# Sine tables from sums of two partial angles, lag matmuls on four column tiles, exponentials first: one change to a two-layer sequence kernel

## The chip, the cores and the metric

The kernel runs on one core of a Trainium2 chip. A core has TensorE (PE; its weight loads are listed as PEld), VectorE (DVE), ScalarE (ACT), GpSimd (POOL) and SyncE (SP), which work through their own instruction streams in order, and 16 DMA engines. DMAs are issued here from the queues of SP, ScalarE and GpSimd. The metric is device time in microseconds (us) for one execution, less is better. Before the change it is 1138.46 us, the median of 7 runs between 1137.23 and 1139.0.

## What is computed

The input `x` has 64 batches, 128 channels and 2048 time steps, in 32-bit floats. Cut to what matters, the reference is

```python
W = weights[condition]                      # one of 16 matrices of 128x128 for each batch
x = x + einsum('bct,bcd->bdt', x, W)        # layer 0
dt = exp(log_dt); A = -exp(log_A_real) + 1j * A_imag; dtA = A * dt[:, None]
Ct = (C[..., 0] + 1j * C[..., 1]) * (exp(dtA) - 1) / A
K = 2 * einsum('hn,hnl->hl', Ct, exp(dtA[:, :, None] * arange(L))).real
y = causal_convolution(x, K) + x * D[:, None]     # by FFT in the reference
x = x + y * mask                            # mask: time step < length of the batch
```

Layer 1 is a linear state-space model: 128 channels h, each with 64 complex modes n. The kernel works with it in chunks of 128 time steps (Q): inside a chunk the output comes from the first 128 values of K as a Toeplitz matrix, and between chunks from states that are carried on.

## The kernel before

It has two stages.

**Stage 1** does layer 0 for the first half of time (1024 steps) and makes the tables of layer 1. A turn of its loop (`now`, 0 to 63) takes one batch (`batch0`, line 464): SP has fetched two batches at a time, 1 MB, into one of ten buffers (`fetch`, line 430; up to nine fetches ahead); GpSimd copies the batch's matrix into a small tile (`weigh`, line 436; three batches ahead, four tiles); TensorE multiplies (`project`, line 448: two matmuls of 512 columns, line 454, into one of two double banks of PSUM); ScalarE copies the result over the input (line 456) and issues its store to a scratch tensor in DRAM (line 459). A buffer is fetched into again when both of its stores have landed. Before turn 12 the parameters of the modes are worked out on DVE, transposed on TensorE (`lay`, line 347) and kept in `gtab`, `ptab` and `wk`; these instructions lie between the first twelve batches, written out by hand.

The tables: the channels are taken in pairs (64 pairs, the two channels' modes on 128 partitions), and pairs in 16 groups of four (TP). For a group `e` holds, for 128 partitions, 4 pairs and 129 steps (NE), the real and imaginary part of a decaying exponential: exp(decay x step) times cosine and sine of an angle. The angle in turns is step x (FHI + FLO) + PHI, where the frequency is kept in two parts for accuracy, and whole turns are taken off by adding and subtracting a large number (MAGIC). The steps of a group in the code:

- `exps` (line 477): four exponentials on ScalarE, 128x129 each. Groups 0 to 3 are done in turns 6 to 9, the others four groups at a time between later batches. Exponentials and sines need different ScalarE function tables; changing them is a table load.
- `angles` (line 590): 16 DVE instructions.
- `sines` (line 617): two ScalarE instructions of 128x516.
- `products` (line 622): two DVE instructions into `e`.
- `lags` (line 631): eight matmuls with weights `wk` of 128x2 and 128 moving columns, which give the 128 lags of K for the group's eight channels as 2 partitions x 4 pairs x 128.
- `keep_lags` (ScalarE copy, line 641), `gain_lags` (line 647, adds 1 + D to lag 0), `store_lags` (line 651, a DMA from GpSimd into the DRAM tensor `kpad`).

From turn 12 on, each turn issues one batch and then six DVE steps of a generator (`tables`, line 688), which goes through the groups as fast as that allows. A small plan (`later`, line 686) places the other engines' steps a fixed number of turns behind. The last groups' steps run over the end of the batches (the loop goes to `B + 9`).

**Stage 2** starts when the scratch tensor is complete: 64 iterations (`iteration`, line 863), each with four channels of one half of time. Per iteration TensorE transposes (line 763), forms the states' inputs (line 788), applies the Toeplitz part (line 829) and the states' part (line 841, on two row tiles of 64 partitions); DVE scans the states (line 803) and writes masked outputs (line 850); SP stores them (`store`, line 856). The second half of layer 0 lies between these as single pieces (`some`, line 662). An iteration's two stores are issued in the iteration after it; those of the last one after the loop.

Of the kernel before, what the change touches and what calls it, by code (L numbers as in the profile page):

```python
# [45 lines left out]
P = 128  # L47
# [16 lines left out]
TP = 4  # L64
# [305 lines left out]
def cond_resid_ssm_kernel(  # L370
# [30 lines left out]
    KP = 2 * Q  # L401
    assert sum(SEGS) == L and set(SEGS) == {SL} and KK == 4
# [11 lines left out]
    kpad = dram.tile([C, KP], F32, tag="kpad", name="kpad")  # L414
    btd = dram.tile([NG, P, GP * 4 * N], F32, tag="btd", name="btd")
# [70 lines left out]
    drow = earlies.tile([2, NP], F32, tag="drow", name="drow")  # L486
# [3 lines left out]
    with tc.tile_pool(name="setup", bufs=1) as setup:  # L490
# [25 lines left out]
        li = setup.tile([P, 1], I32, tag="li", name="li")  # L516
        with nc.allow_non_contiguous_dma(reason="128 gains and 64 lengths"):
            nc.scalar.dma_start(
                drow.rearrange("c (j d) -> c j d", d=2), d_in.rearrange("(j c d) -> c j d", c=2, d=2)
            )  # L520
            for f in range(2):
                nc.scalar.dma_start(li[f * B : (f + 1) * B, :], length.rearrange("(b o) -> b o", o=1))
# [4 lines left out]
        nc.gpsimd.iota(ti, [[1, HL]], base=0, channel_multiplier=0)  # L527

# [8 lines left out]
        def masks():  # L537
            V.tensor_scalar(drow, drow, 1.0, None, ALU.add)
            V.tensor_copy(lf, li)
            V.tensor_copy(steps, stepi)  # L540
            yield
            V.tensor_copy(tf, ti)
            yield
            V.tensor_scalar(tf[B:P], tf[B:P], float(HL), None, ALU.add)
            yield
            for s in range(NS):
                if s:
                    V.tensor_scalar(tf, tf, float(SL), None, ALU.add)
                    yield
                V.tensor_scalar(mask[:, s, :], tf, lf, None, ALU.is_lt)  # L550
                yield
# [37 lines left out]

    def angles(g):  # L590

        t = ts[g] = tmps.tile([P, 2, TP, NE], F32, tag="t", name=f"t_{g}", bufs=4)
        a, r = t[:, 0], t[:, 1]
        for i in range(TP):
            V.tensor_scalar(a[:, i, :], steps, par_of(FHI, g, i), None, ALU.mult)
            yield
        V.tensor_scalar(r, a, MAGIC, MAGIC, ALU.add, ALU.subtract)
        yield
        V.tensor_tensor(a, a, r, ALU.subtract)
        yield  # L600
        for i in range(TP):
            V.tensor_scalar(r[:, i, :], steps, par_of(FLO, g, i), par_of(PHI, g, i), ALU.mult, ALU.add)
            yield
        V.tensor_tensor(a, a, r, ALU.add)
        yield
        V.tensor_scalar(r, a, MAGIC, MAGIC, ALU.add, ALU.subtract)
        yield
        V.tensor_tensor(a, a, r, ALU.subtract)
        yield
        V.scalar_tensor_tensor(r, a, -1.0, a, ALU.mult, ALU.max)  # L610
        later(2, sines, g)
        if g % 4 == 3 and g + 1 < NT:
            for k in range(4):
                later(2 + (k + 1) // 2, exps, g + 1 + k)
        yield
# [6 lines left out]
    def products(g):  # L622
        V.tensor_tensor(es[g][:, :, 1, :], ts[g][:, 0], es[g][:, :, 0, :], ALU.mult)
        yield
        V.tensor_tensor(es[g][:, :, 0, :], ts[g][:, 1], es[g][:, :, 0, :], ALU.mult)
        del ts[g]
        for lag, step in ((3, lags), (4, keep_lags), (6, gain_lags), (8, store_lags)):
            later(lag, step, g)
        yield

    def lags(g):

        pk = ks[g] = psp.tile([2, TP, Q], F32, tag="tr", name=f"pk_{g}", bufs=2)
        for i in range(TP):
            for part in range(2):
                w = wk[:, part, g * TP + i, :]
                nc.tensor.matmul(pk[:, i, :], w, es[g][:, i, part, 1:NE], start=(part == 0), stop=(part == 1))  # L637

    def keep_lags(g):
        krow = tmps.tile([2, TP, Q], F32, tag="krow", name=f"krow_{g}", bufs=3)  # L640
        nc.scalar.copy(krow, ks[g])
        ks[g] = krow

    def gain_lags(g):

        last = ks[g][:, :, Q - 1]
        V.tensor_tensor(last, last, drow[:, g * TP : (g + 1) * TP], ALU.add)

    def store_lags(g):
        h0 = 2 * g * TP  # L650
        nc.gpsimd.dma_start(kpad[h0 : h0 + 2 * TP, 0:Q].rearrange("(p c) q -> c p q", c=2), ks.pop(g))
# [32 lines left out]
    plan = {}  # L684

    def later(lag, step, g):
        plan.setdefault(now + lag, []).append((step, g))

    def tables():
        for g in range(NT + 2):  # L690
            if g < NT:
                yield from angles(g)
            elif g > NT:
                yield from [None] * 12
            if g >= 2:
                yield from products(g - 2)

    making = tables()
    for now in range(12, B + 9):
        if now < B:  # L700
            batch0(now)
        for step, g in plan.pop(now, ()):
            step(g)
        for _ in range(6):
            next(making, None)
        if now == 60:
            fetches(FILL)
    assert not plan and next(making, None) is None
# [147 lines left out]
    def store(i):  # L856
        s, g = seg(i)
        for f in range(2):
            t0 = s * SL + f * HL
            nc.sync.dma_start(out[:, g * CG : (g + 1) * CG, t0 : t0 + HL], xs[i][half[f]])  # L860
        del xs[i]

    def iteration(i):
# [29 lines left out]
        for d in range(GP):  # L893
            if i >= 0:
                outputs(i, d)
            if nxt and d == 0:
# [8 lines left out]
    store(NI - 1)  # L905
# [32 lines left out]
```

## Time and profile before

| | |
|---|---|
| median of 7 runs | 1138.46 us |
| the profiled execution, its own time | 1139.5 us |
| its span | 1137.7 us |
| busy: PE / DVE / ACT / POOL | 1081.1 / 843.0 / 692.8 / 216.5 us |
| granted TensorE clock, mean | 0.99 |
| batch 12's matmuls start | 53.1 us |
| batch 63's matmuls end | 199.5 us |
| batch 63's store lands | 203.4 us |
| the scratch tensor's first load is issued | 203.7 us |

Busy shares are means over two stages. In the page's curves a digit is the busy share of one fortieth of the span (28.4 us) in tenths, 9 for 90% or more, so the first seven digits are stage 1. In the window table each row is a stretch of time, with the busy time of each engine in it and the number of instructions. In the chain of work that ended last each line is a start, a duration, and what the end was waiting for at that time; `x8` counts records, and a 32-bit matmul leaves two of them. In the instruction list a name such as `e<-steps,gtab` says what is written from what.

### The profile page before, as it was taken

To read this page: it belongs to the slowest core of one execution; us is meant where nothing else is said; L and a number is where in the kernel's file an instruction comes from. 1 tells how busy PE (TensorE), PEld (TensorE's weight loads), DVE (VectorE), ACT (ScalarE), POOL (GpSimd) and SP (SyncE) were. 2 spreads that over 40 slices of the span, in tenths; PEclk is the share of its full clock that TensorE was granted. 3 is DMA by queue.
4 is the path that set the end of the run, shared out by engine and by line. 5 is a ranking of instruction groups with operands and counts; after the bars stand their busy time and mean duration, and the time that the engine had idled before them with its cause. 6 is when DMAs were issued, how large, how long until landed. Compare 5 with 4: busy or idle time off the path is not lost.

```text
span 1137.7 us, 23806 instructions
## 1 busy us (share of the span) xinstructions
PE 1081.1 (95%) x8586; PEld 792.3 (70%) x8586; DVE 843.0 (74%) x2811; ACT 692.8 (61%) x1117; POOL 216.5 (19%) x376
## 2 busy tenths in 40 slices
PE   5588889899999999999999999999999999999996
PEld 2233334477777777677777778888888888888885
DVE  7598883266766675676576667888888888888886
ACT  3457785766656656666666666566566566556552
POOL 2012212122222212212222211221121121121120
PEclk9799999999999999999999999999999999999998
DMA  8999998999999999999999977777878787778754
GB/s 316 415 398 372 347 353 312 371 334 291 319 297 291 288 298 309 292 287 305 297 278 296 288 220 226 240 225 222 221 237 225 211 243 227 210 243 227 209 163 111
DMA packets 116793, 313.25 MB, mean 275 GB/s; under 512 B 11428, under 2 KB 11684, under 8 KB 108484
## 3 DMA queue, kind: packets, MB, share of 16 engines
q1 hardware_dynamic: 71184, 219.17, 61.9%
q10 hardware_dynamic: 35764, 67.32, 15.9%
q0 software_dynamic: 9728, 25.25, 8.8%
q8 instruction: 68, 1.11, 0.4%
q14 instruction: 49, 0.40, 0.1%
HBM read 164.76 MB, written 146.93 MB: 274 GB/s over the span
## 4 chain that ended last, share of the span: by engine, by line
PE 87%; DMA 6%; ACT 4%; DVE 1%; issue 1%; ACTq 0%; POOLq 0%; POOL 0%; SPq 0%; DVEq 0%
PE y L841 21%; PE y L829 20%; PE v L788 18%; PE p L454 15%; PE tr L763 10%; DMA xb<-in_x_dram 3%; DMA scr<-xb 2%; PE pk L637 2%; PE pb L745 2%; ACT xb L456 1%; ACT e L480 1%; DVE s L803 1%; DMA x<-scr 0%; ACTq L459 0%; ACT L480 0%
## 5 line engine op out<-in xcount | busy, mean ns | idle before, releaser
L803 DVE SCALAR_TENSOR_TENSOR s<-s,ptab 128x128 f32<-128x128 f32 x1792 | 520.6, 344 | 98.0 <-ACT s L793 80.0
L793 ACT ACTIVATE s<-v,ptab 64x512 f32<-64x512 f32 (+1 forms) x512 | 336.0, 656 | 49.9 <-PE v L788 33.6
L829 PEld LDWEIGHTS y<-tt,u 128*128 128x128 f32 x2048 | 263.5, 192 | 80.5 <-issue 67.0
L454 PE MATMUL p<-xb,w 128*128 128x512 f32 x512 | 255.9, 616 | 38.9 <-ACT xb L456 13.6
L829 PE MATMUL y<-tt,u 128*128 128x128 f32 x2048 | 269.9, 275 | 0.1
L841 PEld LDWEIGHTS y<-e,s 64*128 64x128 f32 x4096 | 233.9, 188 | 46.5 <-issue 24.2
L788 PE MATMUL v<-u,bt 128*128 128x512 f32 (+1 forms) x512 | 248.4, 567 | 0.0
L841 PE MATMUL y<-e,s 64*128 64x128 f32 x4096 | 246.7, 275 | 1.4 <-DVE s L803 1.4
L764 ACT COPY u<-tr 128x512 f32<-128x512 f32 x256 | 150.5, 588 | 153.7 <-PE tr L763 127.4
L812 DVE TENSOR_SCALAR s<-s 128x128 f32<-128x128 f32 x448 | 99.1, 221 | 137.3 <-ACT s L793 137.3
L456 ACT COPY xb<-p 128x512 f32<-128x512 f32 (+1 forms) x192 | 139.1, 725 | 99.3 <-PE p L454 84.0
L850 DVE COPY_PREDICATED x<-mask,y 128x1024 f32<-128x1024 uint8 x128 | 166.6, 1302 | 1.1 <-PE y L841 1.0
L454 PEld LDWEIGHTS p<-xb,w 128*128 128x128 f32 x512 | 88.2, 196 | 112.6 <-issue 82.4
L763 PEld LDWEIGHTS tr<-ident,x 128*128 128x128 f32 x1024 | 121.1, 141 | 51.3 <-issue 44.6
L763 PE MATMUL tr<-ident,x 128*128 128x128 f32 x1024 | 155.6, 274 | 1.0 <-DMA x<-scr 1.0
L446 POOL COPY w<-wres 128x128 f32 x128 | 54.0, 422 | 331.7 <-PE p L454 318.8
L731 POOL DMA_DIRECT2D tt<-kpad x64 | 50.6, 790 | 206.6 <-DVE s L803 166.9
L788 PEld LDWEIGHTS v<-u,bt 128*128 128x128 f32 x512 | 79.6, 191 | 13.9 <-issue 13.6
L746 ACT COPY bt<-pb 128x512 f32<-128x512 f32 x32 | 18.8, 586 | 87.3 <-PE pb L745 86.7
L776 POOL DMA_DIRECT2D s<-carry x64 | 45.0, 708 | 128.1 <-PE y L841 114.3
L820 POOL DMA_DIRECT2D carry<-s x64 | 43.8, 729 | 66.7 <-DVE s L803 62.4
L773 POOL MEMSET s<- 128x384 f32 x32 | 14.8, 462 | 150.4 <-DMA carry<-s 68.9
(169 smaller groups left out, 323.4 us busy)
## 6 DMA issues: line engine op xcount, KB each, us to landing
xb<-in_x_dram SPq DMA_DIRECT2D x64, 1024.0 KB, 9.7
scr<-xb ACTq DMA_DIRECT2D x128, 512.0 KB, 8.0
x<-scr SPq DMA_DIRECT2D x64, 1024.0 KB, 9.2
out_dram<-x SPq DMA_DIRECT2D x128, 512.0 KB, 4.8
tt<-kpad POOLq DMA_DIRECT2D x64, 256.0 KB, 6.3
btd<-bt SPq DMA_DIRECT2D x32, 256.0 KB, 7.9
bt<-btd SPq DMA_DIRECT2D x32, 256.0 KB, 4.9
carry<-s POOLq DMA_DIRECT2D x64, 64.0 KB, 7.1
```

What stands on the lines that cost most here:

```text
L446: nc.gpsimd.tensor_copy(w1s[s, b], wres[:, bass.ds(at, 1), :].rearrange("p s d -> p (s d)"))
L454: nc.tensor.matmul(ps[:, k], w1s[s, b], own[:, cols], start=True, stop=True)
L456: nc.scalar.copy(own[:, cols], ps.rearrange("p k t -> p (k t)"))
L763: nc.tensor.transpose(tr[:, k, :], xs[i][:, c, k * Q : (k + 1) * Q], ident)
L764: nc.scalar.copy(u, tr)
L788: nc.tensor.matmul(v[:, 0:nv], w, us[i, n].rearrange("p k r -> p (k r)")[:, 0:nv], start=True, stop=True)
L793: nc.scalar.activation(own[:, 0:nv], v[lanes, 0:nv], AF.Copy, scale=amp)
L803: nc.vector.scalar_tensor_tensor(new[:, d, 0:2], src, factor, own[:, d, 0:2], ALU.mult, ALU.add)
L812: nc.vector.tensor_scalar(old[:, :, 2], old[:, :, 0], -1.0, None, ALU.mult)
L829: nc.tensor.matmul(y[:, k, :], u[:, k, :], tts[i][:, n, :], start=(k == 0), stop=False, skip_group_check=True)
L841: nc.tensor.matmul(ys[i, d][:, c, k, :], st[half[c], d, part, k, :, :].rearrange("p f b -> p (f b)"), e[half[c], pair % TP, part, 0:Q], st ...
L850: nc.vector.copy_predicated(xs[i][:, d::2, :].rearrange("r c (k t) -> r c k t", k=KK), keep_k.unsqueeze(1).to_broadcast([P, 2, KK, Q]), ys ...
```

## The change

Six things change.

1. **Angles as sums.** A step from 0 to 127 is 16a + b. For each pair, 25 partial angles are worked out once for all groups: 8 for the multiples of 16 (with the phase), 16 for 0 to 15, and one for step 128 (`partial_angles`, in turns 12 to 14: nine DVE instructions of up to 128x1600 and a GpSimd memset of 128x2048). For a group, TensorE transposes its partial angles (`turn_parts`), ScalarE copies them (`keep_parts`), and one matmul with a matrix of zeros and ones (`pick`) adds the two right ones for 4 x 128 steps (`add_parts`). `angles` is then four DVE instructions that take off whole turns and make the second table's absolute value. `pick` is made before turn 12 with six more iotas on GpSimd and four more instructions on DVE.
2. **Lags on column tiles.** The weights are 32 columns (16 pairs' weights, of which those of one pair are wanted), and each of the four pairs of a group has its own 32 output partitions; the wanted rows are then picked by two DMAs.
3. **Exponentials first.** All groups left are done in turns 12 to 17, two groups a turn.
4. **A fixed schedule.** From turn 15 on a group starts every second turn, and each step has its lag in turns (`STEPS`); the loop ends with the batches.
5. **D by rows.** Since lags lie on other partitions, the gains are laid out by two DMAs into DRAM and four out of it, on GpSimd's queue between the third and the fourth batch's weights, in place of one on ScalarE's.
6. **The last store in parts.** The last iteration's outputs are stored pair by pair, one half on SP's queue and the other on ScalarE's.

```diff
             for f in range(2):
-                nc.scalar.dma_start(li[f * B : (f + 1) * B, :], length.rearrange("(b o) -> b o", o=1))
+                nc.scalar.dma_start(lens[f * B : (f + 1) * B, :], length.rearrange("(b o) -> b o", o=1))
...
-            nc.scalar.dma_start(
-                drow.rearrange("c (j d) -> c j d", d=2), d_in.rearrange("(j c d) -> c j d", c=2, d=2)
-            )
+            for c in range(2):
+                nc.gpsimd.dma_start(by_row[c], by_channel[c])
+            for i in range(TP):
+                nc.gpsimd.dma_start(dcol[i * NR : (i + 1) * NR, :], dbyrow.rearrange("(h r) -> r h", r=NR))
...
+    def partial_angles(k):
+        own = parts[:, :, 0:NL]
...
+        if k == 0:
+            nc.gpsimd.memset(parts, 0.0)
+            V.tensor_tensor(own, of(FHI, NL), by_l, ALU.mult)
+            V.tensor_scalar(whole, own, MAGIC, MAGIC, ALU.add, ALU.subtract)
+        elif k == 1:
+            V.tensor_tensor(own, own, whole, ALU.subtract)
+            V.tensor_tensor(whole, of(FLO, NL), by_l, ALU.mult)
+        else:
+            V.tensor_tensor(own, own, whole, ALU.add)
...
+    def turn_parts(g):
+        ps[g] = psp.tile([P, P], F32, tag="tr", name=f"pa_{g}", bufs=2)
+        nc.tensor.transpose(ps[g], parts[:, g * TP : (g + 1) * TP, :].rearrange("p i r -> p (i r)"), ident)
+
+    def keep_parts(g):
+        a = tmps.tile([P, P], F32, tag="a", name=f"a_{g}", bufs=2)
+        nc.scalar.copy(a, ps[g])
+
+    def add_parts(g):
+        ps[g] = psp.tile([P, TP, Q], F32, tag="v", name=f"pt_{g}", bufs=2)
+        nc.tensor.matmul(
+            ps[g].rearrange("p i q -> p (i q)"), a, pick.rearrange("p i q -> p (i q)"), start=True, stop=True
+        )
...
     def angles(g):
-        for i in range(TP):
-            V.tensor_scalar(a[:, i, :], steps, par_of(FHI, g, i), None, ALU.mult)
...
-        V.scalar_tensor_tensor(r, a, -1.0, a, ALU.mult, ALU.max)
+        V.tensor_scalar(r[:, :, 1:NE], ps[g], MAGIC, MAGIC, ALU.add, ALU.subtract)
+        V.tensor_tensor(a[:, :, 1:NE], ps.pop(g), r[:, :, 1:NE], ALU.subtract)
+        V.tensor_copy(a[:, :, 0:1], last[:, g * TP : (g + 1) * TP, :])
+        V.tensor_scalar(r.bitcast(I32), a.bitcast(I32), 0x7FFFFFFF, None, ALU.bitwise_and)
...
     def lags(g):
-        pk = ks[g] = psp.tile([2, TP, Q], F32, tag="tr", name=f"pk_{g}", bufs=2)
-        for i in range(TP):
-            for part in range(2):
-                w = wk[:, part, g * TP + i, :]
-                nc.tensor.matmul(pk[:, i, :], w, es[g][:, i, part, 1:NE], start=(part == 0), stop=(part == 1))
+        pk = ks[g] = psp.tile([P, Q], F32, tag="tr", name=f"pk_{g}", bufs=2)
+        pairs = slice(g // 4 * 16, g // 4 * 16 + 16)
+        for part in range(2):
+            for i in range(TP):
+                w = wk[:, part, pairs, :].rearrange("p k c -> p (k c)")
+                nc.tensor.matmul(
+                    pk[i * NR : (i + 1) * NR, :], w, es[g][:, i, part, 1:NE], start=(part == 0), stop=(part == 1)
+                )
...
     def store_lags(g):
-        nc.gpsimd.dma_start(kpad[h0 : h0 + 2 * TP, 0:Q].rearrange("(p c) q -> c p q", c=2), ks.pop(g))
+        for c in range(2):
+            r0 = g % 4 * 8 + c
+            nc.gpsimd.dma_start(to[c], krow[r0 : r0 + 3 * 34 + 1 : 34, :])
...
-    for now in range(12, B + 9):
-        if now < B:
-            batch0(now)
-        for step, g in plan.pop(now, ()):
-            step(g)
-        for _ in range(6):
-            next(making, None)
+    FIRST = 15
+    STEPS = {12: store_lags, 10: gain_lags, 8: keep_lags, 7: lags, 6: products,
+             4: sines, 3: angles, 2: add_parts, 1: keep_parts, 0: turn_parts}
+    for now in range(12, B):
+        batch0(now)
+        if now < FIRST:
+            partial_angles(now - 12)
+        if now < 18:
+            exps(2 * now - 20)
+            exps(2 * now - 19)
+        for lag, step in STEPS.items():
+            g, odd = divmod(now - FIRST - lag, 2)
+            if not odd and 0 <= g < NT:
+                step(g)
...
-    def store(i):
+    def store(i, d=None):
         s, g = seg(i)
-        for f in range(2):
+        own = slice(0, CG) if d is None else slice(d, CG, 2)
+        for f, queue in ((0, nc.sync), (1, nc.sync if d is None else nc.scalar)):
             t0 = s * SL + f * HL
-            nc.sync.dma_start(out[:, g * CG : (g + 1) * CG, t0 : t0 + HL], xs[i][half[f]])
-        del xs[i]
+            queue.dma_start(out[:, g * CG : (g + 1) * CG, t0 : t0 + HL][:, own], xs[i][half[f], own])
...
             if i >= 0:
                 outputs(i, d)
+            if not nxt:
+                store(i, d)
...
-    store(NI - 1)
```

In turn n the steps stand behind the batch, oldest group first, so a group's first transpose is in turn 15 + 2g, its angle matmul in turn 17 + 2g, its lag matmuls in turn 22 + 2g and its stores in turn 27 + 2g; the last stores are in turn 57.

## The prediction

> **What bounds the kernel now.** I read the two-line load curve first, then a table of time windows, then the chain that ended last, then the instructions of one stretch in order of time. Everything the change touches, the last store apart, lies in stage 1, which ends when batch 63's store has landed (203.4 us). After it TensorE is the bound.
>
> ```profile
> PE   5588889899999999999999999999999999999996
> DMA  8999998999999999999999977777878787778754
> ```
>
> DMA is nearly full in stage 1 too, so the question is which of the two sets its pace. The window table (us, then busy time of PE, PEld, DVE, ACT, POOL, then the TensorE clock, DMA share, GB/s):
>
> ```profile
> 53.00:77.00 24.00, 19.57 (x42) 8.10 (x41) 22.64 (x57) 11.38 (x13) 3.45 (x9) 0.92 1.03 395
> 86.00:104.00 18.00, 13.56 (x44) 5.49 (x41) 15.30 (x37) 15.78 (x31) 3.79 (x7) 1.00 1.02 379
> 104.00:117.00 13.00, 13.00 (x56) 6.41 (x56) 12.41 (x33) 8.19 (x11) 4.01 (x8) 1.00 1.00 360
> 117.00:131.00 14.00, 9.26 (x43) 4.30 (x40) 12.33 (x32) 12.95 (x26) 2.24 (x5) 1.00 1.01 376
> 131.00:150.00 19.00, 18.96 (x63) 8.95 (x64) 17.02 (x39) 11.44 (x16) 4.60 (x10) 0.91 0.93 343
> 150.00:165.00 15.00, 10.31 (x46) 4.56 (x44) 11.83 (x31) 13.56 (x26) 1.73 (x5) 1.00 0.94 335
> 165.00:200.00 35.00, 34.95 (x138) 16.97 (x139) 13.79 (x32) 20.93 (x27) 8.09 (x20) 1.00 0.87 317
> ```
>
> PE is full in three of these and idle by 4.4, 4.7 and 4.7 us (13.9 together) in three others. Those three are the bursts in which ScalarE makes four groups of exponentials between its copies:
>
> ```profile
> 150.60 1.28 ACT L480 ACT_TABLE_LOAD   x1
> 151.89 1.28 ACT L480 ACTIVATE e<-steps,gtab 128x129 f32<-128x129 f32 x4
> 154.51 2.45 ACT L480 ACTIVATE e<-steps,gtab 128x129 f32<-128x129 f32 x8 [0.44 <-ACT xb L456]
> ```
>
> So from batch 23 (its matmuls start at 80.8) to the end of batch 63 (199.5) PE is the bound wherever ScalarE is not. DMA is not: batch 40's input lands at 98.4 and is used at 133.9. The chain says the same, and shows what the reader needs of prices (start, us, what):
>
> ```profile
> 79.06 1.85 PE pk L637 x16
> ...
> 192.47 7.08 PE p L454 x16
> 199.57 1.02 ACT xb L456
> 200.61 2.81 DMA scr<-xb
> 203.66 5.14 DMA x<-scr
> ...
> 232.86 3.77 PE y L841 x64
> 237.66 0.89 PE y L829 x8
> ```
>
> **The change, part by part.** Turn n is the loop turn that projects batch n. A batch costs PE 1.84 us (3.67 for two in the chain), ScalarE 1.01 for its copy and 0.44 until its next work.
>
> *DVE.* A group's angles go from 16 instructions to four, its products stay: about 7.6 us (L595 to L625) become some 3.6. This is worth nothing by itself: PE is full at DVE 95% (104 to 117) and at DVE 39% (165 to 200).
>
> *PE per group.* Removed: eight matmuls of 2 columns, 1.85. Added: one transpose, 0.15 (L763: four in 0.60); one 512-wide matmul, 0.92 (half of a batch); eight 32-column matmuls on four column tiles, which no row shows. Bounds: 2.05 if tiles run one after another and each change of tiling costs 0.1 (L841's first records last 373 ns against 272), 0.45 if four run at once. The nearest row is L841: 64 records on two row tiles at 59 ns each, against 111 for L829 on the whole array, so tiles do overlap. I take 0.65 (0.45 and two changes). Together 1.72 against 1.85.
>
> [...]
>
> *Front: exponentials in turns 12 to 17.* Batch 12's copy starts at 56.8. Each of six turns then holds ScalarE for 1.01 + 0.44 + 2.57 (eight exponentials at 0.32) = 4.02, with one table load of 1.28 and one small copy of 0.3: batch 18's copy starts at 82.4, where it now starts at 71.6. PE follows: batch 16 waits for copy 14, and the first angle matmul stands before batch 18 and waits for the copy of its operand, queued behind turn 16's exponentials (78.4). Angle matmuls 1 and 2 wait likewise (84.1, 89.8). Batch 22 runs at 90.9, the first lag matmuls behind it, batch 23 at 93.4: 12.6 later than now. POOL's memset (some 2.5: L773 takes 0.46 for 384 columns) and the nine DVE instructions of the partial angles (about 10) end near 66; the first transpose needs them, but batch 16 waits for copy 14 until 67.1 anyway. Without that cover they would cost about 1. SP's fetches wait for stores, so they come later too; inputs are 20 us and more ahead here (batch 18 lands at 44.7 and is used at 68.6), so nothing waits for them.
>
> *Before turn 12.* The gains D move from ScalarE's queue to POOL's: two DMAs, a wait for their landing, four more, then eight iotas, all ahead of the fourth batch's weights, now copied at 13.3. Six issues at 0.55 (L651), a landing of 5 (kpad's is 1.8 to 5.9 and the lengths' took up to 8.2), iotas 2.5: these weights come at 24, batch 3 at 24.4 for 19.0, and the transposes behind it at 26.5, which DVE wants at 24.8. With 1.4 for the picking matrix DVE is 3.1 late. The cover: DVE now waits 4.9 for the next transpose, which stands behind batch 9, and that for stores behind fetches. The `+ 1` of the gains on DVE waits for the second round of these DMAs, out by 21 and landed near 26; DVE comes to it at 30. If the cover is gone, all 3.1 count. I take 1.0, between -1 (one small DMA less ahead of the first fetches) and 6.
>
> *Back.* From 94.4: 41 batches 75.4, 13 angle matmuls 12.0, 12 transposes 1.8, 15 groups of lags at 0.65, 9.8: 99.0. The idle 13.9 has no cause left, since ScalarE's two turns need 2 x 1.45 + 1.34 (sines) + 0.6 (two small copies) = 4.8 against PE's 5.4. But data is asked for at 384 GB/s (1.05 MB per 2.73 us), and the most that windows show with loads and stores alike is 395. A store waits on ScalarE until the DMA before it on its one of eight semaphores has landed (the store at 67.06 left when a fetch had landed at 66.98, and the copy behind it came 4.4 late), so a full queue stops the copies. I add 2.5, between 0 and 14 (the idle of the same stretch now). Batch 63 then ends at 195.9 instead of 199.5: -3.6.
>
> *POOL's stores of lags*: 32 issues for 16, 9 us more beside 78% idle; six turns old data, so nothing. The weights behind them are three turns early.
>
> *The end.* Now, after the last DVE instruction:
>
> ```profile
> 1128.72 1.29 DVE L850 COPY_PREDICATED x<-mask,y 128x1024 f32<-128x1024 uint8 x1 [0.48 <-PE y L841]
> 1130.04 1.25 SPq L860 DMA_DIRECT2D out_dram<-x  x2
> ```
>
> Two stores of 512 KB, the second landing at 1136.5. After: half of it leaves 1.8 earlier, and the rest is two of 256 KB on two queues. A store of 512 KB lands in 4.8 (median), 64 KB from carry in 3.9, so the end gains between 0.6 (5.8 as now, one issue saved) and 2.6. I take 1.8.
>
> **Sum.** -3.6 - 1.8 = -5.4 on the profiled execution's 1139.5 (span 1137.7, 1.8 around it): 1134.1. That execution stands 1.0 above the median of seven, 1138.5, so 1133.1.
>
> **Rivals.** Forecasts as medians.
>
> 1. *Column tiles don't overlap (slower).* [...] Against: L841. At 2.05 the 15 groups cost 21 us more: 1154. It decides from 1.0 us per group: there 15 x 0.36 eats the whole 5.4. 18%.
> 2. *The front costs more*: D's round trip not covered (+5), and PE, idle in pieces of 3 us, at a lower clock (0.75 between 40 and 60 us now): up to 1142. Against: DMA stays full there. 15%.
> 3. *PE is faster than I counted*: lags at 0.45 (-3), transposes in shadow, no idle (-2.5), -1 at the start: 1126. Against: DMA at 395. 12%.
> 4. *Stage 1 doesn't move*, since DMA sets it: from 53 to 77 it moves 395 GB/s, from 77 to 200 a mean of 350, 52.5 MB together. If 350 is all that it gives when loads and stores alternate, the same bytes end at the same time however PE is filled, and only the end gains: 1136.7. Against: inputs lie ready 35 us ahead, which a queue that is the bound would not leave. 10%.
>
> **How the numbers follow.** The forecast, with its bounds 1129 to 1137, has 45%. From no change (1138.5) 0.2%, or 2.3 us, can be told. Faster: 0.9 of the forecast, case 3, a little of 4: 0.55. Same: the rest of 4 and of the forecast, a third of 2: 0.16. Slower: case 1 and most of 2: 0.29. The range reaches from 1125 (case 3) to 1149, into case 1 where tiles overlap by a quarter (lags near 1.7), and leaves out its upper end.
>
> **What would show it.** Lag matmuls: eight in about 0.65. PE full from 95 us to batch 63's end near 196; batch 18's copy near 82; batch 3 near 24. The last store lands about 4.3 after the last DVE instruction. I am wrong if lags last over 1 us, if PE has gaps after 100 us while ScalarE waits to issue stores, or if turn 12 starts later than 57.

## Result, and the profile after

The changed kernel takes 1143.8 us (median of 17 runs, 1137.9 to 1149.4) beside 1138.8 us for the kernel before on the same chip (43 runs, 1136.7 to 1141.6): ratio 1.0037, interval 1.0027 to 1.0047. Two repetitions gave 1.0019 (1.0004 to 1.0033) and 1.0031 (1.0017 to 1.0045). So it is slower by 2 to 5 us, where 5.4 us less were forecast. The profiled execution is one of the quicker ones, 1139.25 us (span 1137.5), 0.25 below the one of before.

The page's two load curves of the changed kernel (tenths, 40 slices of 28.4 us):

```profile
PE   2779999899999999999999999999999999999996
DMA  8999999989999999999999977778777788787764
```

PE's first slices fell from 5, 5, 8, 8 to 2, 7, 7, 9. The window table (us; busy PE, PEld, DVE, ACT, POOL; granted clock, DMA share, GB/s):

```profile
20.00:30.00 10.00, 0.61 (x2) 0.50 (x2) 4.33 (x31) 2.86 (x4) 5.38 (x16) 0.71 0.86 239
53.00:77.00 24.00, 17.24 (x31) 6.86 (x31) 13.74 (x29) 15.67 (x36) 5.47 (x6) 0.72 0.96 349
77.00:95.00 18.00, 12.29 (x26) 4.80 (x26) 5.17 (x10) 14.74 (x32) 1.49 (x5) 0.91 0.90 334
...
117.00:131.00 14.00, 13.07 (x75) 5.49 (x74) 8.82 (x20) 9.37 (x16) 5.50 (x11) 1.00 1.03 388
...
165.00:180.00 15.00, 15.00 (x79) 6.50 (x78) 5.06 (x11) 9.96 (x14) 5.08 (x13) 1.00 1.04 405
180.00:190.00 10.00, 8.96 (x21) 3.56 (x20) 0.16 (x1) 5.23 (x6) 3.47 (x9) 1.00 1.04 412
190.00:200.00 10.00, 9.50 (x23) 3.97 (x22) 0.00 (x0) 6.14 (x7) 1.78 (x6) 1.00 1.05 406
```

PE works 0.6 us between 20 and 30 us, has gaps up to 95, and is nearly full from there. DMA has changed places with it: the rows before 95 lost rate (395 GB/s between 53 and 77 us became 349), and the end of stage 1, which ran at 317 GB/s, is full at 405 to 412. Batch 23 starts at 97.5 us (80.8 before), batch 63's matmuls end at 197.3 (199.5).

The chain that ended last (start, duration, what):

```profile
13.50 10.53 DMA dbyrow<-in_L_cond_D_dram
...
26.27 0.22 POOLq L444
...
29.12 0.32 POOL w L451
29.48 3.78 PE p L459 x4
...
171.31 7.42 DMA scr<-xb
178.80 8.06 DMA xb<-in_x_dram
...
188.51 8.84 PE p L459 x20
...
199.92 3.43 DMA scr<-xb
203.53 5.45 DMA x<-scr
209.11 1.09 PE tr L826 x4
```

D's transfer stands in it with 10.5 us, and at the end of stage 1 transfers that were not in it before. 2.2 us gained on PE at batch 63 are 0.1 us at the scratch tensor's first load (203.53 for 203.66), since batch 63's store, issued at 198.41, landed at 203.25: 4.84 us for 2.81. (The chain's line at 199.92 names the store issued after it, which was still under way; the load waits for batch 63's.) The instructions of PE in order of time, changed kernel:

```profile
96.89 0.65 PE L691 MATMUL pk<-e,wk 128*32 128x128 f32 x16
...
209.11 1.09 PE L826 MATMUL tr<-ident,x 128*128 128x128 f32 x4 [3.39 <-DMA x<-scr]
209.99 1.91 PE L459 MATMUL p<-xb,w 128*128 128x512 f32 x2
```

The lags last 0.65, as forecast. Between the stages PE stands 3.4 us for the scratch tensor (1.0 before), and then two records of 512 columns, 1.02 to 1.10 elsewhere, take 1.91: the granted clock is 0.88 from 204 to 210 us and 0.84 from 210 to 216. The states' matmuls begin at 234.3 for 232.8. From there to the last DVE instruction it is 897.22 us in both profiles: whatever stage 1 and the passage to stage 2 lose is in the time.

### The profile page after: what moved, and what is told of

The parts are those of the page before. It is cut to its first block, busy times and chain, and to the rows that moved or that the text cites. A ratio compares the mean times of both kernels' runs of the same rounds, so it can differ in the third digit from the quotient of the medians.

```text
span 1137.5 us, 23839 instructions
## 1 busy us (share of the span) xinstructions
PE 1081.5 (95%) x8634; PEld 787.1 (69%) x8634; DVE 793.1 (70%) x2664; ACT 686.7 (60%) x1129; POOL 228.9 (20%) x405
## 4 chain that ended last, share of the span: by engine, by line
PE 85%; DMA 5%; ACT 4%; DVE 2%; issue 1%; ACTq 1%; POOL 0%; POOLq 0%; SPq 0%; DVEq 0%
PE y L904 21%; PE y L892 20%; PE v L851 18%; PE p L459 13%; PE tr L826 10%; DMA xb<-in_x_dram 2%; DMA scr<-xb 2%; ACT xb L461 2%; PE pb L808 2%; ACT e L485 1%; DMA dbyrow<-in_L_cond_D_dram 1%; PE pt L661 1%; DVE s L866 1%; ACTq L464 1%; DMA x<-scr 0%
## 5 line engine op out<-in xcount | busy, mean ns | idle before, releaser
L856 ACT ACTIVATE s<-v,ptab 64x512 f32<-64x512 f32 (+1 forms) x512 | 335.9, 656 | 50.5 <-PE v L851 34.0
L459 PE MATMUL p<-xb,w 128*128 128x512 f32 x512 | 260.8, 623 | 30.2 <-POOL w L451 23.4
L459 PEld LDWEIGHTS p<-xb,w 128*128 128x128 f32 x512 | 88.6, 199 | 99.9 <-issue 60.6
```

The lines of the kernel that those rows point to most:

```text
L459: nc.tensor.matmul(ps[:, k], w1s[s, b], own[:, cols], start=True, stop=True)
L856: nc.scalar.activation(own[:, 0:nv], v[lanes, 0:nv], AF.Copy, scale=amp)
```

## Experiments

The theories, in the order in which they came up. **1**: GpSimd's wait for D's round trip through DRAM makes turn 12 late. **2**: exponentials in turns 12 to 17 starve PE. **3**: the DMA queue is full at the end of stage 1 and takes what PE gains. **4**: PE runs dry between the stages, and its clock falls. **5**, formed on the way: D's two transfers into DRAM stop the DMA engines themselves.

### The changed kernel twice more

> The changed kernel once more, unaltered, as the measure for the three runs beside it and for a second profile of it. Theory 1 (the wait of POOL for D's round trip through DRAM shifts turn 12): the landing of the two first DMAs (10.5 us in the first profile) differs between executions; batch 12 starts at 57.7 plus or minus some 3, and the time follows it; ratio to the kernel before 1.003 to 1.006. Theory 2 (exponentials in turns 12 to 17 starve PE) has no reason for a changing time: batch 12 and batch 23 stay at 57.7 and 97.5 within 0.5. Theory 3 (the DMA queue is full at the end of stage 1): batch 63's store lands more than 4 us after its issue again, and idle of PE between 104 and 200 us is above 3 us again.

> The changed kernel unaltered, as the measure for the three beside it: ratio to the kernel before 1.002 to 1.004, batch 12 at 57.5 to 58.2.

The three profiles put batch 12 at 57.7, 58.2 and 57.0, batch 23 at 97.5, 97.9 and 96.7, and the end of batch 63 at 197.3, 200.6 and 194.9. So batch 12 stays within 1.2 us, and what varies is the 98.3 to 102.7 us from batch 23 on, where ScalarE's waits for a semaphore held by a DMA sum up to 10.1 to 12.0 us from 104 us on. In two of the three the last iteration also took 1.6 us more: 40 records of states at 4.13 us for 2.50, at a clock of 0.5 to 0.67. Of this 0.8 us came back, since the last store then landed 3.9 us after the last DVE instruction for 4.65. Why executions differ so is not settled.

### D: the wait, or the transfer

D's first two DMAs as GpSimd's first work:

```diff
...
+        for c in range(2):
+            nc.gpsimd.dma_start(by_row[c], by_channel[c])
         make_identity(nc, ident)
...
-            for c in range(2):
-                nc.gpsimd.dma_start(by_row[c], by_channel[c])
             for i in range(TP):
                 nc.gpsimd.dma_start(dcol[i * NR : (i + 1) * NR, :], dbyrow.rearrange("(h r) -> r h", r=NR))
```

> The changed kernel with the first two DMAs of D (gains into DRAM by rows) issued as POOL's first work, before the inputs of stage 1 are asked for; the four reads back stay where they are. POOL's wait of 10.5 us goes, the fourth batch's weights come at about 17 instead of 29, and batch 3 and what stands behind it on PE come 8 to 10 us earlier. Theory 1: batch 12 comes at 53 to 54 instead of 57.7, all of stage 1 behind it moves by the same 4, and the time falls by 3.5 to 5 us against the changed kernel, with less scatter. Theory 2: turns 12 to 17 are bound by ScalarE, which starts with them 4 earlier too, so it says the same 4 for this run, but batch 23 less batch 12 stays at 39.7 us. Theory 3: batch 63's matmuls come earlier but its store lands at the same 203.3, since the same bytes pass a full queue: under 1 us.

Measured: 1.0026 (1.0015 to 1.0037), no gain. GpSimd's wait was gone (the fourth weights at 18.0), but the first batch's input landed at 16.1 instead of 11.9, and batch 12 came at 55.5. A miss for theory 1. What the next runs show in other places is here ahead of the first input: with these two DMAs under way, the engines moved 27 to 105 GB/s between 10 and 13.5 us.

The six DMAs and the wait alone, in the kernel before:

```diff
...
+            for c in range(2):
+                nc.gpsimd.dma_start(by_row[c], by_channel[c])
+            for i in range(TP):
+                nc.gpsimd.dma_start(dcol[i * 32 : (i + 1) * 32, :], dbyrow.rearrange("(h r) -> r h", r=32))
             for f in range(2):
                 nc.scalar.dma_start(li[f * B : (f + 1) * B, :], length.rearrange("(b o) -> b o", o=1))
```

> The kernel before with one thing of the change added: D's six DMAs on GpSimd's queue between the third and the fourth batch's weights, with the wait between them (the gains are also loaded as before; the new tile is only added to, and not used). Theory 1: the two first DMAs land about 10 us after their issue, the fourth batch's weights come at 26 to 28 for 13.3, batch 3 at 26 to 28 for 19.0, batch 12 at 56 to 57.5 for 53.1, and since PE sets the rest of stage 1 in this kernel, batch 63 ends 2 to 4.5 us later and the time is 2 to 4.5 us more. Rival (the front has slack that the prediction's 1.0 stood for): under 1 us.

1.0049 (1.0036 to 1.0062), 5.8 us: this one part costs more than the whole change. Batch 3 at 27.9, batch 12 at 57.9, batch 63's end at 205.4.

D out of the way of GpSimd's weights, in the changed kernel (the two DMAs after batch 4, the four in turn 14):

```diff
...
             batch0(b)
+            if b == 4:
+                gains_out()
...
+        if now == 14:
+            for i in range(TP):
+                nc.gpsimd.dma_start(dcol[i * NR : (i + 1) * NR, :], dbyrow.rearrange("(h r) -> r h", r=NR))
+        if now == 20:
+            V.tensor_scalar(dcol, dcol, 1.0, None, ALU.add)
```

> The changed kernel with D's DMAs out of the way: the two first on GpSimd's queue after batch 4, the four others in turn 14, the addition of 1 in turn 20 (the first use is in turn 25). Unlike the run with D as the first work, nothing is put ahead of the first input (that run's first batch started 4.1 us later, 16.17 for 12.05, so that it exchanged one wait for another). Theory 1: the fourth batch's weights come at 15 to 17, batch 3 at about 19, batch 12 at 53 to 54 for 57.7, and the time falls by 3 to 5.8 us against the changed kernel (the last is what the wait alone cost the kernel before). Theory 3 (the queue sets the end of stage 1): the DMA hole between 20 and 30 us (239 GB/s) is filled too, which is 1.6 MB or 4 us of a full queue, so 2 to 4 us. If neither: under 1 us.

1.0008 (0.9997 to 1.0018), under its control by 1.6 us in the medians and 2.6 in the ratios. Batch 3 came in time (18.9), but batch 12 still at 56.6, so GpSimd's wait was not what made it late. The view of the DMA engines from 10 to 50 us (one figure per us) shows what was. First the kernel before, then the changed kernel, then D late:

```profile
GB/s 89 258 406 353 382 424 418 430 406 320 315 346 406 424 420 410 416 416 420 410 424 412 426 410 422 406 430 408 422 412 422 410 420 416 414 418 416 414 416 412
```

```profile
DMA  9999999992936986799979999999999999999999
GB/s 397 410 399 429 414 414 426 402 209 74 106 106 158 223 180 131 289 410 420 370 286 416 422 418 408 414 422 422 416 418 412 418 412 418 408 426 416 420 408 416
...
dbyrow<-in_L_cond_D_dram POOLq DMA_DIRECT2D x2, 0.2 KB, 8.8
```

```profile
GB/s 393 414 405 418 414 418 410 410 410 414 397 410 408 424 416 412 402 72 39 59 47 82 156 137 338 412 406 418 424 408 422 412 428 406 428 404 422 420 414 414
```

From some 5 us after the issue of the two DMAs of 64 values of 4 bytes, until about their landing, all 16 engines together move 39 to 223 GB/s for 7 to 8 us. The hole moves with them: from 18 to 26 us in the changed kernel, where they are issued at 12.8 and 13.5, from 27 to 34 with D late (21.5 and 22.2). The last two runs put this to the test. The two DMAs alone, in the kernel before, with no reader:

```diff
             batch0(b)
+            if b == 4:
...
+                for c in range(2):
+                    nc.gpsimd.dma_start(by_row[c], by_channel[c])
             run(phases, 12)
```

> The kernel before with only D's two first DMAs (128 gains of 4 bytes each from DRAM to DRAM) on GpSimd's queue after batch 4; nothing reads them and nothing waits for them. Theory 1 (GpSimd's wait is the cost): no wait, so the time is the kernel before's within 1 us, ratio 0.999 to 1.001. Theory 5 (formed on the run with D late, where batch 3 came in time but batch 12 was still 3.4 us late: while these two DMAs are under way, the 16 DMA engines move 25 to 70 GB/s for some 6 us instead of 410, wherever they stand): DMA falls below 100 GB/s for about 6 us near 27 to 33 us, stores land later, ScalarE waits for them, batch 12 comes 3 to 4 us later and the time is 3 to 5.8 us more, ratio 1.0025 to 1.005.

1.0052 (1.0038 to 1.0066), 5.9 us: as much as with the wait. The same DMA view:

```profile
GB/s 123 324 397 347 387 414 426 422 410 324 309 399 418 416 420 412 349 324 92 27 57 76 53 92 252 193 377 416 412 420 424 410 410 422 418 416 414 420 418 420
DMA packets 4536, 13.25 MB, mean 331 GB/s; under 512 B 419, under 2 KB 547, under 8 KB 4535
...
dbyrow<-in_L_cond_D_dram POOLq DMA_DIRECT2D x2, 0.2 KB, 12.5
```

In the 40 us it moved 13.25 MB, the kernel before 15.79: 2.54 MB are 6.1 us at 415 GB/s, and the time is 5.9 us more. ScalarE's waits in this run (18 to 60 us: in total, times, longest) show how it reaches PE, since a copy stands behind a store that cannot be issued:

```profile
ACT xb L457 <- DMA xb<-in_x_dram: 8.9, 1, 8.9
ACT L481 <- DMA scr<-xb: 4.2, 1, 4.2
```

Batch 12 came at 58.4. Theory 1 falls: nobody waited for D here. Theory 5 holds.

The kernel before has a small hole of its own: from 9.9 to 11.4 us it moves 92 GB/s. The six profiles of kernels with the old load of D (128 values into two partitions, on ScalarE's queue) have 92 to 153 GB/s there; the eleven without it, and without D as the first work, have 395 to 415. If the load makes it, which no run tests by itself, the changed kernel's +4.6 us at batch 12 are a net figure.

### Exponentials

One group in each of turns 12 to 23, table groups four turns later:

```diff
-    FIRST = 15
+    FIRST = 19
...
-        if now < 18:
-            exps(2 * now - 20)
-            exps(2 * now - 19)
+        if now < 24:
+            exps(now - 8)
```

> The changed kernel with one group of exponentials in each of turns 12 to 23 instead of two in each of turns 12 to 17; the table groups start four turns later (19 for 15), so that sines come after all exponentials and the number of table loads stays. Theory 2: ScalarE needs 1.45 + 1.28 = 2.7 per turn, two turns 5.5 for two batches against 8.0 now; batch 18 comes near 74 instead of 84, batch 23 near 87 instead of 97.5 less 16 spared work that comes later, and if PE is the bound of the rest the time falls by 3 to 8 us. Theory 3: PE catches up earlier but then waits for DMA; batch 63's store lands at 203.3 still, and the time moves by less than 1 us. Theory 1: batch 12 stays at 57.7 and the end of stage 1 gains nothing that DMA had not.

0.9987 (0.9975 to 1.0000) beside 1.0019 for the changed kernel in the same runs: 3.6 us. Batch 18 at 74.2 and batch 23 at 89.4 for 84.5 and 97.9. Theory 2 holds, at the lower end of its 3 to 8 us; theory 3's under 1 us is a miss. With both this and D first:

> Both edits of the two runs before together. Theory 1 and 2 together: batch 12 at 53 to 54, batch 23 at 83 to 85, stage 1 ends 5 to 10 us earlier than in the changed kernel, near 194 to 198; time 1131 to 1137. Theory 3: stage 1's last store lands at 202 to 203 whatever is done, and the time is within 1 us of the better of the two single edits.

0.9995 (0.9983 to 1.0007), no better; batch 63's matmuls ended at 196.0 in this run, with single exponentials and with D first alike, though batch 23 lay between 89.0 and 95.0. That the two gains do not add up speaks for theory 3.

The reverse, exponentials first in the kernel before:

```diff
-        if g % 4 == 3 and g + 1 < NT:
-            for k in range(4):
-                later(2 + (k + 1) // 2, exps, g + 1 + k)
...
             batch0(now)
+        if now < 18:
+            exps(2 * now - 20)
+            exps(2 * now - 19)
```

> The kernel before with one thing of the change: all exponentials left in turns 12 to 17, two groups a turn, and none later; angles, lags, D and the end as before. Theory 2 (exponentials first starve PE, and with it the DMA queue, between 60 and 95 us): batch 18 at about 80 for 68.6, batch 23 at 90 or later for 80.8; DMA falls to about 300 GB/s between 70 and 90 us; the idle of PE in the later bursts of exponentials (13.9 us) goes, but what DMA did not move is moved at the end of stage 1, where it was not full (195 GB/s at 192 to 198 us): batch 63's end within 2 us of 199.5, on either side. If PE alone set stage 1, the end would come at 199.5 + 10 - 13.9, at 195.6 or before, and the time 3 to 4 us lower.

1.0005 (0.9996 to 1.0015). Its window table:

```profile
80.00:90.00 10.00, 7.20 (x8) 2.35 (x8) 7.89 (x19) 9.01 (x16) 0.76 (x2) 0.54 0.69 253
90.00:100.00 10.00, 9.97 (x41) 4.83 (x42) 7.63 (x21) 6.23 (x9) 1.55 (x5) 1.00 0.87 295
120.00:170.00 50.00, 49.96 (x202) 23.93 (x200) 47.75 (x119) 31.88 (x42) 15.40 (x26) 1.00 1.04 412
```

Batch 23 came 14.7 us later, at a DMA rate down to 253 GB/s and a clock of 0.54; then PE had no idle at all while DMA moved 412 GB/s for 50 us, and batch 63 ended at 198.6 for 199.5. Loss in front and gain behind cancel, so exponentials first are no gain in themselves. It also shows that a full DMA queue need not stop PE.

### The end, and the passage between the stages

The last stores in parts alone, in the kernel before (the diff's `store(i, d)` and its two calls):

> The kernel before with one thing of the change: the last iteration's outputs stored pair by pair on two queues. The prediction's step says -1.8 us (1136.7 against 1138.5), the last stores landing 4.3 to 4.7 us after the last DVE instruction for 6.4 now. Rival: the two queues share the same DMA engines and the end waits for a fixed completion time, then -0.6 at most.

0.9983 (0.9973 to 0.9993), -1.6 us in the medians and -1.9 in the ratio, beside the forecast's -1.8; the last store lands 4.7 us after the last DVE instruction for 6.4.

Twelve pieces for eight between the stages, with single exponentials:

```diff
-    some(8)
+    some(12)
```

> The changed kernel with single exponentials as in the run on exponentials above, and twelve instead of eight pieces of the second half of layer 0 between stage 1 and the first iteration (the four come out of the iteration before the first). Theory 4 (PE runs out of work while the scratch tensor makes its round trip, idles 3.4 us, its clock drops, and the first iteration starts 1.5 us late): the pieces fill 205.7 to 209.1, the clock stays at 1.00, the first states' matmuls of stage 2 come 29.1 us or less after the scratch tensor's first load is issued instead of 30.7, and the time falls by 1.5 to 4 us against single exponentials alone (0.9987 of before: to 0.995 to 0.997). Rival: the four pieces' copies on ScalarE and their input, still on its way, hold up the first iteration as much as they save: within 0.5 us.

0.9967 (0.9955 to 0.9979): 2.3 us under single exponentials alone, though in other runs. The states' matmuls came 29.3 us after the scratch tensor's first load was issued, for 30.7. The same edit in the kernel before, with its last stores in parts:

> The kernel before with the last iteration's stores pair by pair (as in the run on that alone, 0.9983) and twelve instead of eight pieces between the stages. Theory 4: in this kernel PE is idle for 1.0 us only before the first transposes (208.9) and its clock is full there, so the pieces fill little: between no gain and 1.0 us over the stores alone, ratio 0.9975 to 0.9985. Rival (moving the pieces out of the iteration before the first is itself the gain of 2 us seen with single exponentials): 0.996 to 0.997.

1.0010 (1.0002 to 1.0019): no gain, but 3 us lost to the stores alone. The first transposes came 2.9 us after their input had landed, behind the pieces, and the 29.1 us became 31.8. Theory 4 holds for the sign: pieces pay where PE is dry for 3.4 us and cost where it is dry for 1.0; that they cost so much was a miss.

Its second half, the clock, is shown less well. With eight pieces, PE stood 2.1 us before the first transposes in the first repetition, 2.8 with single exponentials and 3.6 in the second repetition, and the granted clock was 0.72 in the 6 us from there in all three. With D first it stood 2.9 us, the clock stayed at 1.00, and the states' matmuls still came 30.9 us after the load's issue, since later transposes waited 0.97 us for a copy of ScalarE. With D late and single exponentials (below) it stood 1.8 us, at a clock of 1.00, and they came after 29.3 without the four pieces. So in the changed kernel's own profile the half-speed records are there to see, but a full clock alone would not have saved the 1.6 us in every execution. With D first and twelve pieces:

> The changed kernel with single exponentials, the two first DMAs of D as POOL's first work, and twelve pieces between the stages. Theory 4: with the idle of PE between the stages filled, what comes earlier in stage 1 is no longer given back, so the 1.5 to 2 us of D's wait, which showed in the profiles but not in the medians, show: 0.995 to 0.996 of before. Theory 3 (the queue sets the end of stage 1): as with twelve pieces and D's wait, 0.9967 within 0.001.

0.9981 (0.9969 to 0.9992): D as the first work again won nothing.

### Column tiles, and stores from GpSimd

The order of the eight lag matmuls changed, neighbours on one tile:

```diff
-        for part in range(2):
-            for i in range(TP):
+        for i in range(TP):
+            for part in range(2):
```

> The changed kernel with the eight lag matmuls of a group in another order: both parts of one pair, then of the next, so that neighbours go to the same column tile. If tiles overlap only when neighbours lie on different tiles, a group's lags last 1.2 to 1.9 us for 0.65, PE has 9 to 19 us more work in stage 1; if PE sets the end of stage 1 the time is 7 to 15 us more, if the DMA queue sets it (theory 3) under 4. If the order does not matter (0.65 again), the time is the changed kernel's within 1 us.

1.0027 (1.0015 to 1.0038), the changed kernel's own. PE's instructions in this run:

```profile
96.51 0.67 PE L691 MATMUL pk<-e,wk 128*32 128x128 f32 x16
```

The four tiles' first records start 12 to 14 ns apart (6 to 7 in the changed kernel), and each tile's next record 0.11 to 0.13 us after. Tiles overlap in either order.

Stage 1's stores issued by GpSimd, with single exponentials:

```diff
-            nc.scalar.dma_start(to, own.rearrange("c (f t) -> c f t", f=2))
+            (nc.gpsimd if s == 0 else nc.scalar).dma_start(to, own.rearrange("c (f t) -> c f t", f=2))
```

> The changed kernel with single exponentials, and stage 1's stores issued from GpSimd's queue instead of ScalarE's, so that a store whose semaphore is still in use holds up GpSimd, which has three turns in hand, and not the copies. Theory 3 in its strict form (DMA moves all it can, waits of ScalarE are only where that shows): batch 63's store lands at 201.3 within 1 us as with single exponentials alone, and the time within 1 us of that run's 0.9987. Rival (the waits themselves cost, since copies and with them PE stand still 1 to 4 us at a time while DMA has other work): PE has no gaps after 100 us, batch 63 ends 2 to 4 us earlier, and the time falls by 1.5 to 4 us.

1.0054 (1.0039 to 1.0070), a miss for both. Up to 100 us it did what the rival said: DMA at 419 to 420 GB/s from 60 to 100, batch 23 at 81.5 instead of 89.4. Then the lags' stores, which GpSimd issues too, stood behind the others, and ScalarE waited for the lags' three buffers (110 to 200 us):

```profile
ACT krow L697 <- DMA kpad<-krow: 22.0, 8, 5.1
```

### Versions

D late and single exponentials, without and with twelve pieces:

> D late as in the run beside it, and single exponentials in turns 12 to 23. Theories 1 and 2 add: batch 12 at 53 to 54, batch 23 near 85, time 5 to 8 us below the changed kernel (ratio to the kernel before 0.995 to 0.998). Theory 3: PE waits again behind 100 us, and it stays within 1 us of single exponentials alone (0.9987).

> As the run beside it with twelve pieces between the stages. Theory 4: another 2 us, since stage 1's earlier end would otherwise be idle of PE between the stages: ratio 0.992 to 0.995. If stage 1's end is set by the queue, 0.9967 as with D's wait.

0.9986 (0.9970 to 1.0002) and 0.9956 (0.9939 to 0.9972). By the first, D late adds nothing to single exponentials (0.9987 in other runs), as is to be expected if the hole in the DMA rate only moves; why it won 1.6 to 2.6 us without them is open. The second is 3.4 us below the first. In the two profiles, 2.9 us apart, only 1.0 of that lies behind the scratch tensor's first load (28.3 for 29.3); the rest is stage 1, where the two kernels are the same, so part of it is spread between executions. Last, the gains straight into their partitions (the diff shows this part alone):

```diff
-                nc.gpsimd.dma_start(by_row[c], by_channel[c])
...
+        if 13 <= now < 13 + TP:
+            i = now - 13
+            own = dcol[i * NR : (i + 1) * NR, :]
+            for d in range(2):
+                for c in range(2):
+                    nc.gpsimd.dma_start(
+                        own[2 * d + c : NR : 4, :], d_in.rearrange("(h j c d) -> c d j h", j=8, c=2, d=2)[c, d]
+                    )
```

> As the run with D late, single exponentials and twelve pieces (0.9956), but the gains are loaded straight from the input into their 128 partitions by sixteen DMAs of 32 values on GpSimd's queue in turns 13 to 16, without the round trip through DRAM. Theory 5: no collapse of the DMA rate before turn 12, batch 12 at 53 to 54 for 56.3, and the time 2 to 4 us less: ratio 0.992 to 0.994, 1130 us or below. Rival (sixteen small DMAs collapse the queue as the two did, only later; or the end of stage 1 takes the gain): 0.995 to 0.997.

1129.9 us for 1139.2: 0.9925 (0.9912 to 0.9939), faster than both kernels, and 3.5 us below the version with D late in other runs (0.9956). Its profiled execution is the quickest of its seven (1124.5). Its DMA view from 10 to 50 us:

```profile
GB/s 414 427 403 403 439 401 414 414 418 406 397 401 424 414 414 410 424 426 404 414 426 420 412 408 420 422 416 406 420 418 426 406 416 420 426 401 406 410 420 422
DMA packets 5578, 16.58 MB, mean 415 GB/s; under 512 B 336, under 2 KB 464, under 8 KB 5575
```

No hole, neither that of the two DMAs nor the old one between 9.9 and 11.4 us; batch 12 at 50.5, earlier than in the kernel before (53.1), batch 63's end at 185.8. The sixteen DMAs of 32 values run between 55 and 73 us, where single slices of 0.5 us fall to 230 GB/s, but most stay near 400.

## Why the prediction was wrong

The sum against the profiled execution, by the prediction's own steps (us). The first three rows make up the fourth; the last sums the fourth to the seventh. The stretch from batch 23 on is its "Back":

| step | forecast | measured | with |
|---|---|---|---|
| before turn 12 | +1.0 | +4.6 | batch 12 at 57.7 for 53.1 |
| front, batch 12 to batch 23 | +12.6 | +12.0 | 39.75 for 27.7 |
| batch 23 to batch 63's end | 101.5 | 99.9 | (118.7 before) |
| batch 63's end | -3.6 | -2.2 | 197.3 for 199.5 |
| its store and the issue after it | 0 | +2.1 | store 4.84 for 2.81 |
| passage to the states' matmuls | 0 | +1.6 | 30.8 for 29.1 |
| the end | -1.8 | -1.8 | 4.65 for 6.44 |
| sum | -5.4 | -0.3 | 1139.25 for 1139.5 |

**The step that failed is "Before turn 12".** It had D's DMAs as a wait of GpSimd with a landing of 5 us, covered by DVE's 4.9; they landed in 10.5, and the cost was not the wait. The two transfers into DRAM hold up every other transfer for some 8 us (74 to 223 GB/s from 18 to 26 us, for 397 to 429 between 10 and 18). The sign that the prediction named, turn 12 later than 57, came (57.7). Alone they cost the kernel before 5.9 us, at the upper bound of 6 that the text kept. The rows taken for the landing (kpad, the lengths) told how long a small DMA takes, not what the others do meanwhile. Rival 2 named this place ("D's round trip not covered, +5") at 15%, with the wrong mechanism. That 1143.8 lies in the stated range of 1125 to 1149 is luck: rival 2 went up to 1142, and what lies above was there for rival 1, which fell.

**Two steps were missing from the sum.** Batch 63's end was carried to the end of the kernel as it stood. But the bytes that had not moved before 95 us moved at the end of stage 1, where the queue had moved 317 GB/s (165 to 200 us): the last store took 2.0 us longer. And PE, earlier by 2.2 us, stood dry for 3.4 us between the stages, ran its next records at half speed (1.91 us for 1.02) and began stage 2 later by 1.6. With twelve pieces beside single exponentials this is 29.3 for 30.7; how much of it is the clock stays open, since D first lost as much at a full clock. This is half of rival 4: DMA did not set stage 1's whole length, but it took the gain at its end.

**Right:** PE per group (lags 0.65, angle matmuls and transposes as priced), the front's +12.6 from ScalarE, the end's -1.8 (alone -1.6). Rival 1 fell outright: the weight loads of the four tiles start within 20 ns of each other, and the eight matmuls took 0.65 for its 2.05. "Back" was right in size, 101.5 for 98.3, 99.9 and 102.7 in three profiles, partly because two errors cancel: in the first profile PE was busy 96.0 us for the 99.0 counted and idle 3.9 for the 2.5 added for ScalarE's waits at the store issues. The sign it named for being wrong, PE gaps after 100 us while ScalarE waits, is there (117 to 131, 150 to 165 and 180 to 190 us).

**Open:** the median of the changed kernel lies 2 to 5 us above the kernel before, while this profile shows -0.3. The two other profiles show the spread, in the stretch from batch 23 to 63 and in the last iteration's clock, but not what decides it; the version without the hole still spreads over 7 us (1124.5 to 1131.4). Nor do the parts add up exactly: D alone +5.9, exponentials first +0.7, stores in parts -1.6 make +5.0 for the first three, which by difference leaves 0 to -3 for angles as sums, column tiles and the fixed schedule together; these weren't run by themselves. Nor was the changed kernel with nothing but D's load mended.

## What to carry to other kernels

Price a new DMA by what the other transfers do while it is under way, not only by who waits for it: where the queue is full, look at the rate in slices of 1 us, and try a scatter of single values once alone. When a gain is carried through a stage boundary, add what the last transfer, and the engine that then runs dry, do with it. A stretch of work that is moved to the front is paid in idle of everything behind it (exponentials first in the kernel before: batch 23 14.7 us later); it is worth something only if the idle it removes later is longer (there batch 63's end came 0.9 earlier).

## What the runs showed of the hardware

- Two DMAs of 64 values of 4 bytes from DRAM to DRAM, written at every second value, brought the 16 engines from 410 to between 27 and 92 GB/s for 6 us, while their busy share, in windows of 2 us, was 0.70 and more (in the run with them alone). Sixteen DMAs of 32 such values into partitions did not (between 54 and 74 us a mean of 377, the lowest slice of 0.5 us at 230). Whether it is the target, the stride or the number of values in one transfer wasn't tried by itself. The old load of D, 128 such values into two partitions, goes with 92 to 153 GB/s for 1.5 us in six profiles, which speaks against DRAM as the target being all of it. These runs show the slowness for 4 bytes into DRAM, not its mechanism.
- Four column tiles of 32 columns overlap almost fully in fp32: 16 records in 0.65 us, where the same number on one tile took 1.85 (the 2-column lags before). Their weight loads, 0.11 us each, start within 20 ns of each other, and the order of issue doesn't matter (0.67 with neighbours on one tile).
- After 3.4 us without work two of PE's records of 512 columns took 1.91 us for 1.02, and the mean clock was 0.88 from 204 to 210 us and 0.84 from 210 to 216. Pauses of 2.1, 2.8 and 3.6 us in three other profiles were followed by a clock of 0.72 over 6 us, one of 2.9 us by 1.00: the length of the pause alone does not decide. In the last iteration, after three pauses of 0.47 us, two profiles of three show a clock of 0.5 to 0.67 and the third 1.00. Why like pauses end differently, no run here shows.
